# Cross-attention on one core: queries of two batches projected together with inner block products, context product plain, keys' affine folded into the queries'

## Chip, core and metric

The kernel runs on one NeuronCore of a Trainium2 chip. The metric is the device time in microseconds of one execution. Engines: TensorE (PE; its weight loads are shown apart as PEld), VectorE (DVE), ScalarE (ACT), GpSimd (POOL), and SyncE (SP), which issues nearly all DMA transfers. Each engine, SP's queue too, works through its instructions in the order in which the program lists them.

## The reference

64 batches of cross-attention, float32 throughout: x is (64, 256, 512), the context c is (64, 256, 384).

```python
text_p  = einsum('bld,dh->blh', x, W_text) + b_text        # queries, 512 -> 512
audio_p = einsum('bsd,dh->bsh', c, W_audio) + b_audio      # keys and values, 384 -> 512
Q = layer_norm(text_p, g1, beta1)
K = layer_norm(audio_p, g2, beta2)
V = audio_p
alpha = softmax(einsum('blh,bsh->bls', Q, K) / sqrt(512), axis=-1)
y = einsum('blh,hk->blk', einsum('bls,bsh->blh', alpha, V), W_out) + b_out
return layer_norm(y + x, g_out, beta_out)
```

## The kernel before

**Products.** A batch has five matrix products on TensorE. W_audio and W_out are folded once into `wao` (384 x 512), so the values are never formed: the context product takes the attention weights with the raw rows of c, and the output product takes that with `wao`.

- Keys (class `Thirds`): a scheme of 15 block products in place of 18 (weights 128x171), in methods `one` (2 products), `two` (2), `three` (1), `four` (5), `five` (5). They accumulate in PSUM areas M, L, T, U, N; between them VectorE and ScalarE move partial sums from area to area (`copy_n1`, `start_t`, `copy_t`, `start_l0`, `start_l1`, `take_m`, `start_u`). The sums of input blocks (`Sides`, tile csum) are made on GpSimd, one `cs[..].add(1)` each.
- Queries (class `Fork`): seven block products in place of eight (Strassen's idea in Winograd's form), each of two 128-row parts with 256 columns: methods `one` to `seven`. They share two PSUM banks (`fork`) with partial sums: `after_one`, `after_seven` and `seed` on ScalarE, `start_q3`, `step_r`, `after_five` on VectorE. `SumX` makes four sums of x blocks on GpSimd.
- Scores (class `Attention`): seven block products of 128 columns for eight (`score_part`), with sums of query and key blocks on GpSimd (`query_step`, `key_step`). Three batches at the start and two at the end use the plain product (`score`).
- Context: the first two of three 128-row groups of c by seven products of 128 columns (`z_part`, L1033) with sums `c_step` and `e_step` on GpSimd, copies `keep_z7`, `copy_z1`, `copy_top` on ScalarE, additions `add_u3`, `add_c22`, `add_c21` on VectorE; the third group plain (`context_two`, L1095).
- Output: the 15-product scheme again (object `y`), fed by `z_step` sums; its last sums (`plus_ends`, `plus_middle`, `plus_n0`, `last_..`) add x and give the row totals for the layer norm.

**Between products.** Queries and keys are normalised by rows on ScalarE (`square`, `scales_of`, `normalise`), stored to DRAM and fetched back as 32x32 squares (`store`, `fetch`: four transfers), so that VectorE's 32x32 transposes (`turn`) give their transposes; the attention weights go the same way (`store_e`, `fetch_e`, `turn_e`). x and c are fetched as squares as well (`turn_x`, `turn_c`). After the turn ScalarE applies gain and bias per column: four `affine_queries` and four `affine_keys` a batch (L527). The last layer norm is `totals`, `deviation`, `shift` (VectorE), `settle` (VectorE).

**Order.** The program is scheduled by hand: every method call is a line, and the lines of several batches are interleaved. The main loop runs over b = 3 to 60, one batch an iteration, and holds in one iteration the keys and queries of batch b+2, the scores of b, context and output of b-2, and the last layer norm of b-3. A long list of lines ahead of the loop and one after it treat the first and last batches. Score, context and third-group tiles share two PSUM banks in turn (`p_at`).

Of the kernel before, what the change touches and what calls it, by code (L numbers as in the profile page):

```python
# [22 lines left out]
def kernel(  # L23
# [34 lines left out]
    blk = ctx.enter_context(tc.tile_pool(name="blk", bufs=2))  # L58
    work = ctx.enter_context(tc.tile_pool(name="work", bufs=2))
# [26 lines left out]
    def load_x(b):  # L86
        xq = blk.tile([P, L // SQ, D // NQ], F32, tag="xq", name=f"xq_{b}")
        squares(xq, x[b])
        blocks[b].append(xq)
# [15 lines left out]
    make_identity(nc, ident)  # L105
    eps = const.tile([P, 1], F32, tag="eps", name="eps")
# [43 lines left out]
    blocks = {}  # L150
# [4 lines left out]
    columns = const.tile([P, 5, HC], F32, tag="columns", name="columns")  # L155

# [32 lines left out]
    class RowTurn:  # L189

        def __init__(self, rows_sb, chunks, name):
            self.rows, self.chunks = rows_sb, chunks
            tag = "yr" if chunks == DC else "kT"
            self.ar = work.tile([P, 2, chunks, P], F32, tag=tag, name=f"{name}r")
            self.T = work.tile([P, chunks, 2 * P], F32, tag=name, name=f"{name}_0")
# [8 lines left out]

    waT = []
# [75 lines left out]
    def weight_sums(w_sb, n, name):  # L281

        w = [[w_sb[:, j * n : (j + 1) * n, k * H2 : (k + 1) * H2] for k in (1, 0)] for j in (0, 1)]
        t = const.tile([P, 4, n, H2], F32, tag=name, name=name)
        add = nc.gpsimd.tensor_tensor
        add(t[:, 0], w[0][1], w[0][0], ALU.subtract)
        add(t[:, 1], w[1][1], t[:, 0], ALU.subtract)
        add(t[:, 2], w[1][1], w[0][1], ALU.subtract)
        add(t[:, 3], w[1][0], t[:, 1], ALU.subtract)
        ws = {1: w[0][0], 2: w[1][0], 3: w[1][1], 4: t[:, 3], 5: t[:, 0], 6: t[:, 1], 7: t[:, 2]}  # L290
        return {p: [ap[:, k, :] for k in range(n)] for p, ap in ws.items()}

    class SumX:

        def __init__(self, xT, engine=nc.gpsimd):
            n = DC // 2
            part = lambda i, j: xT[:, j * n : (j + 1) * n, bass.ts(i, P)]
            s = work.tile([P, 4, n, P], F32, tag="xsum", name="xsum")
            self.engine = engine
            self.steps = [  # L300
                (s[:, 2], part(0, 0), part(1, 0), ALU.subtract),
                (s[:, 0], part(1, 0), part(1, 1), ALU.add),
                (s[:, 1], s[:, 0], part(0, 0), ALU.subtract),
                (s[:, 3], part(0, 1), s[:, 1], ALU.subtract),
            ]
            ss = {
                1: part(0, 0), 2: part(0, 1), 4: part(1, 1),
                5: s[:, 0], 6: s[:, 1], 7: s[:, 2], 3: s[:, 3],
# [3 lines left out]
        def add(self, n=4):  # L312
# [114 lines left out]
    class Projection:  # L427
# [72 lines left out]
        def fetch(self):  # L500
            self.sq = blk.tile(
# [215 lines left out]
    class Fork(Projection):  # L717

        R, q1 = fork[0][:, :H2], fork[0][:, H2:]
        q2, q3 = fork[1][:, :H2], fork[1][:, H2:]  # L720
# [6 lines left out]
        @staticmethod  # L727
        def seed():
            nc.scalar.copy(Fork.R, bt_sb[:, H2:])

        def product(self, n, place):
            for c, (side, w) in enumerate(zip(self.sides[n], self.weights[n])):
# [4 lines left out]
                    start=(n == 7 and c == 0),  # L737
# [7 lines left out]
        def seven(self):  # L745
            self.product(7, self.q3)
# [4 lines left out]
        def after_seven(self):  # L751
            self.s7 = once.tile([P, H2], F32, tag="s7", name="s7")
            nc.scalar.copy(self.s7, self.q3)
# [4 lines left out]
        def start_q3(self):  # L758
            dve(self.q3, self.R, self.s7, ALU.add)

        def step_r(self):
            dve(self.R, self.R, bt_step, ALU.add)

        def after_six(self):
            self.start_q3()
            self.step_r()
# [4 lines left out]
        def after_five(self):  # L771
            dve(self.q2, self.R, self.s7, ALU.add)
# [7 lines left out]
        def four(self):  # L780
            self.product(4, self.q3)

        def rest(self):
            self.three()
            self.two()
            self.four()
# [18 lines left out]

    class Attention:
# [7 lines left out]
        def affine_queries(self, *chunks):  # L814
            self.q.affine(g1_sb, be1_sb, chunks or range(HC))

# [54 lines left out]
        def open_scores(self):  # L871

            self.sc = p_at.tile([P, LT, S], F32, tag="at", name="ps_sc")
            nc.vector.memset(self.sc[:, :, P:], 0.0)
# [91 lines left out]
        def fetch_e(self):  # L966
            self.sq = blk.tile([P, L // SQ, S // NQ], F32, tag="eq", name=f"eq_{self.b}")
# [18 lines left out]
        def context_sums(self):  # L986

            rows = c_rows[self.b]
            a = lambda j, s: rows[:, s, bass.ts(j, P)]
            t = once.tile([P, 3, P], F32, tag="asum", name="asum")  # L990
            self.csteps = [
                (t[:, 0], a(1, 0), a(1, 1), ALU.add),
                (t[:, 2], a(0, 0), a(1, 0), ALU.subtract),
                (t[:, 1], t[:, 0], a(0, 0), ALU.subtract),
                (a(1, 0), a(0, 1), t[:, 1], ALU.subtract),
            ]
            self.asides = {
                1: a(0, 0), 2: a(0, 1), 3: a(1, 0), 4: a(1, 1), 5: t[:, 0], 6: t[:, 1], 7: t[:, 2],
            }

        def weight_sums(self):

            t = once.tile([P, 4, P], F32, tag="esum", name="esum")
            b = lambda i, m: self.eT[:, i, bass.ts(m, P)]
            self.esteps = [
                (
                    t[:, 0:2],
                    self.eT[:, :, P:],
                    self.eT[:, 0].rearrange("p (m l) -> p m l", m=2),
                    ALU.subtract,  # L1010
                ),
                (t[:, 2], b(1, 1), t[:, 0], ALU.subtract),
                (t[:, 3], b(1, 0), t[:, 2], ALU.subtract),
            ]
            self.bsides = {
# [1460 lines left out]
```

## Time and profile before

| | |
|---|---|
| time, median of 3 runs | 1336.47 us (1336.44 to 1337.37) |
| span of the profiled execution, first to last instruction | 1333.9 us |
| what lies around the span, to the median of the runs | 2.6 us (the profiled execution's own time is not given beside its span) |
| PE busy | 1327.5 us, 8497 matmul records |
| PEld, DVE busy | 1246.6 us, 1257.0 us |
| ACT, POOL busy | 1174.8 us, 1172.8 us |
| granted TensorE clock | 1.000 |
| DMA | 322.23 MB, 242 GB/s |

The span is one execution. A float32 matmul appears as two records, as it passes through the array twice. In the groups of instructions a row gives line, engine, operation, output<-inputs, shapes, count, then busy time in us and the mean length of one in ns, then idle time ahead of it. The mean includes the part by which neighbours overlap, the busy time does not.

### The profile page before, as it was taken

The numbers are of one execution on the slowest core, as the hardware profiler recorded it, in microseconds if no ns is written. First come the engines' busy times: TensorE is split into PE (matmuls) and PEld (weight loads), VectorE is DVE, ScalarE is ACT, GpSimd is POOL, SyncE is SP. The second block draws the span as 40 slices with busy tenths as digits, with TensorE's granted clock in tenths as the row PEclk, the third lists the DMA queues.
The fourth block names the chain that finished last, engine by engine and source line by source line (L and its number), as shares of the span: only waits on it lengthen the run. The fifth ranks groups of instructions, "written<-read, shape, count | busy, mean of one in ns | idle before, by whom it ended". The sixth has DMA issues, their size and how long they took to land.

```text
span 1333.9 us, 29733 instructions
## 1 busy us (share of the span) xinstructions
PE 1327.5 (100%) x8497; PEld 1246.6 (93%) x8497; DVE 1257.0 (94%) x3314; ACT 1174.8 (88%) x3310; POOL 1172.8 (88%) x1854
## 2 busy tenths in 40 slices
PE   9999999999999999999999999999999999999998
PEld 5899999999999999999999999999999999999996
DVE  6769999999999999999999999999999999999977
ACT  4899898898898998998988988989988989889886
POOL 5789999999998998998999999989989989999964
PEclk9999999999999999999999999999999999999999
DMA  9988898898988988988888988988889888889783
GB/s 214 250 235 239 230 268 238 241 261 237 250 251 225 261 248 241 259 248 244 249 241 239 264 236 246 260 241 246 252 225 268 246 236 258 242 241 257 213 248 116
DMA packets 448970, 322.23 MB, mean 242 GB/s; under 512 B 153765, under 2 KB 381349, under 8 KB 448806
## 3 DMA queue, kind: packets, MB, share of 16 engines
q1 hardware_dynamic: 448710, 320.20, 85.7%
q8 instruction: 68, 1.11, 0.4%
q14 instruction: 96, 0.79, 0.2%
q10 hardware_dynamic: 96, 0.13, 0.0%
HBM read 203.57 MB, written 116.65 MB: 240 GB/s over the span
## 4 chain that ended last, share of the span: by engine, by line
PE 98%; DMA 1%; DVE 0%; SPq 0%; issue 0%; POOL 0%; ACT 0%; DVEq 0%
PE ps_f L733 29%; PE ps_m L557 16%; PE ps_sc L884 14%; PE ps_n L557 11%; PE ps_u L557 8%; PE ps_z L1033 7%; PE ps_l L557 5%; PE ps_z L1095 5%; PE ps_sc L823 1%; DMA ba<-in_L_xattn_b_audio_dram 0%; DMA c<-in_ctx_dram 0%; PE ps_l L244 0%; PE ps_f L440 0%; PE ps_fold L244 0%; PE ps_m L244 0%; PE ps_sc L900 0%
## 5 line engine op out<-in xcount | busy, mean ns | idle before, releaser
L352 POOL TENSOR_TENSOR csum<-csum,cT 128x256 f32<-128x256 f32 x310 | 202.0, 652 | 0.6
L733 PE MATMUL ps_f<-wtsum,xsum 128*128 128x256 f32 x756 | 194.0, 379 | 0.0
L527 ACT ACTIVATE qT<-qT,columns 128x256 f32<-128x256 f32 x256 | 152.9, 599 | 0.0
L733 PEld LDWEIGHTS ps_f<-wtsum,xsum 128*128 128x128 f32 x756 | 131.8, 191 | 11.4 <-issue 0.7
L869 POOL TENSOR_TENSOR qsum<-qT 128x256 f32<-128x256 f32 x118 | 86.4, 732 | 58.3 <-ACT qT L527 56.7
L1158 ACT ACTIVATE junk<-yr,nm 128x512 f32<-128x512 f32 x124 | 88.6, 715 | 55.0 <-POOL nm L1140 54.8
L527 ACT ACTIVATE kT<-kT,columns 128x256 f32<-128x256 f32 x256 | 133.7, 595 | 0.4 <-DVE kT L76 0.4
L884 PE MATMUL ps_sc<-kT,qT 128*128 128x128 f32 x928 | 131.8, 275 | 0.0
L733 PE MATMUL ps_f<-wt,xT 128*128 128x256 f32 x504 | 129.5, 379 | 0.0
L1357 DVE SCALAR_TENSOR_TENSOR yr<-yr,rstd,beo 128x512 f32<-128x512 f32 x120 | 123.0, 1025 | 0.1
L884 PEld LDWEIGHTS ps_sc<-kT,qT 128*128 128x128 f32 x928 | 121.3, 192 | 0.0
L1348 DVE SCALAR_TENSOR_TENSOR yr<-yr,nm,go 128x512 f32<-128x512 f32 x124 | 109.7, 885 | 0.0
L794 ACT ACTIVATE junk<-ps_f 128x512 f32<-128x512 f32 x126 | 75.2, 597 | 35.7 <-PE ps_f L733 32.2
L884 PEld LDWEIGHTS ps_sc<-ksum,qsum 128*128 128x128 f32 x696 | 100.6, 191 | 6.0
L884 PE MATMUL ps_sc<-ksum,qsum 128*128 128x128 f32 x696 | 105.8, 275 | 0.0
L733 PEld LDWEIGHTS ps_f<-wt,xT 128*128 128x128 f32 x504 | 88.4, 190 | 6.7
L314 POOL TENSOR_TENSOR xsum<-xT 128x256 f32<-128x256 f32 x124 | 91.0, 735 | 1.9 <-DVE xT L76 1.9
L541 DVE TENSOR_TENSOR ps_l<-ps_m,t 128x171 f32<-128x171 f32 x248 | 82.8, 334 | 8.7 <-ACT t L605 3.0
L520 DVE STREAM_TRANSPOSE kT<-kq 128x512 f32<-128x512 f32 x122 | 85.4, 702 | 2.0 <-DMA kq<-kd 2.0
L488 ACT ACTIVATE kr<-kr,rstd 128x512 f32<-128x512 f32 x126 | 84.7, 727 | 0.0
L460 ACT ACTIVATE junk<-kr 128x512 f32<-128x512 f32 x126 | 80.9, 642 | 0.3
L804 ACT ACTIVATE qr<-ps_f,rstd 128x512 f32<-128x512 f32 x126 | 80.2, 690 | 0.2
(302 smaller groups left out, 4670.1 us busy)
## 6 DMA issues: line engine op xcount, KB each, us to landing
kd<-kr SPq DMA_DIRECT2D x64, 512.0 KB, 3.4
kq<-kd SPq DMA_DIRECT2D x256, 128.0 KB, 3.8
qd<-qr SPq DMA_DIRECT2D x64, 512.0 KB, 3.2
qq<-qd SPq DMA_DIRECT2D x256, 128.0 KB, 4.3
xq<-in_x_dram SPq DMA_DIRECT2D x252, 128.0 KB, 2.8
x<-in_x_dram SPq DMA_DIRECT2D x63, 512.0 KB, 5.0
out_dram<-yr SPq DMA_DIRECT2D x62, 512.0 KB, 3.8
cq<-in_ctx_dram SPq DMA_DIRECT2D x252, 96.0 KB, 2.4
```

What stands on the lines that cost most here:

```text
L314: self.engine.tensor_tensor(*step)
L352: nc.gpsimd.tensor_tensor(*step)
L520: nc.vector.transpose(self.T.rearrange("p k (q t j) -> p t q k j", t=self.nt, j=SQ)[:, t], self.sq[:, t * NQ : (t + 1) * NQ].rearrange("p ...
L527: nc.scalar.activation(self.T[:, k, :], self.T[:, k, :], AF.Identity, bias=bet[:, k : k + 1], scale=gam[:, k : k + 1],)
L557: nc.tensor.matmul(place, lhsT=self.sides.of[n], rhs=self.weights[n], start=(n == 14), stop=True, skip_group_check=True,)
L733: nc.tensor.matmul(place, lhsT=side, rhs=w, start=(n == 7 and c == 0), stop=True, skip_group_check=True,)
L869: nc.gpsimd.tensor_tensor(*self.steps[n])
L884: nc.tensor.matmul(self.place(t, m), lhsT=self.qsides[n][:, c], rhs=self.ksides[n][:, c], start=False, stop=True, skip_group_check=True,)
L1033: nc.tensor.matmul(self.zp[{1: 0, 2: 0, 4: 2}.get(n, 1)], lhsT=self.asides[n], rhs=self.bsides[n], start=(n == 7), stop=True, skip_group_c ...
L1158: nc.scalar.activation(junk, self.y[:, t, :], AF.Square, bias=self.nm[:, t : t + 1], accum_out=self.ssq[:, t : t + 1],)
L1348: nc.vector.scalar_tensor_tensor(row, row, self.nm[:, t : t + 1], go_sb, ALU.add, ALU.mult)
L1357: nc.vector.scalar_tensor_tensor(self.y[:, t, :], self.y[:, t, :], self.r[t], beo_sb, ALU.mult, ALU.add)
```

## The change

- Batches 6 to 63 are projected in pairs (class `Pair`); batches 1 to 5 keep `Fork`, which now uses another form of the same scheme. Of the seven products of a pair three (2, 3, 4) are `whole`: two batches, two parts, 256 columns. The other four (1, 5, 6, 7) are done by seven inner products each, 128 columns wide (`multiply(m, n)`), with sums of sides on GpSimd (`sum`, `side`), inner sums of weights made once (`inner_weights`), and, for each of the four, a `seed`, a `spread` and a `keep` on ScalarE and two `plus` on VectorE. Between the products lie `keep_v`, `keep_s7` and three `leave` (ScalarE), `raise_v`, two `plus_v` and `leave_11` (VectorE). The rows of the queries go to SBUF before `square` and `normalise`.
- The context product is plain for all batches (`context_part`, `copy_one`): no `z_part`, `c_step`, `e_step`, and none of the copies and additions with them.
- From batch 3 on the keys get no affine, up to the last two batches: the queries' gain and bias are multiplied by the keys' gain (`both`, `affine_both`). What the keys' bias would add is the same for all keys of a query and drops out of the softmax.
- The main loop runs over b = 4, 6, .. 58, two batches an iteration. In it one of the two `settle` of a batch becomes `scale_row` (ScalarE) and `lift_rows` (GpSimd), and `open_scores` clears with ScalarE in place of a memset on VectorE.
- The landing rooms of fetched queries, keys and attention weights (tags qq, kq, eq) have one buffer in place of two; the transposed x lies in one fixed room for two batches (`X`), and the sums of both in `xsums`.
- The lists of lines ahead of, in and after the loop are in a new order.

```diff
-            self.sq = blk.tile(
+            self.sq = sq1.tile(
...
+    class Pair:
+
+        A, B = [f.rearrange("p (i h) -> p i h", i=2) for f in fork]
+        room = xsums.rearrange("p i n c l -> p (i n c l)")
+        T = room[:, : 3 * H].rearrange("p (n i c l) -> p n i c l", n=3, i=2, c=2)
+        I = room[:, 3 * H : 3 * H + 3 * P].rearrange("p (n l) -> p n l", n=3)
+        x00, x01 = X[:, :, 0:2, :P], X[:, :, 2:4, :P]
+        x10, x11 = X[:, :, 0:2, P:], X[:, :, 2:4, P:]
+        bank = {1: A, 7: A, 6: B, 5: B}
+        sides = {1: x00, 5: T[:, 0], 6: T[:, 1], 7: T[:, 2], 2: x01, 3: x11, 4: x10}
...
+        def sum(self, n):
+            o, i0, i1 = {
+                1: (self.T[:, 0], self.x10, self.x00),
+                3: (self.T[:, 2], self.x11, self.x10),
+                2: (self.T[:, 1], self.x11, self.T[:, 0]),
+                4: (self.x10, self.x01, self.T[:, 1]),
+            }[n]
+            nc.gpsimd.tensor_tensor(o, i0, i1, ALU.subtract)
+
+        def side(self, m, k):
+            y = self.sides[m]
+            o, i0, i1 = [
+                (self.I[:, 0:2], y[:, 1], y[:, :, 0]),
+                (self.I[:, 2], y[:, 1, 1], self.I[:, 0]),
+                (y[:, 1, 0], y[:, 0, 1], self.I[:, 2]),
+            ][k]
+            nc.gpsimd.tensor_tensor(o, i0, i1, ALU.subtract)
...
+        def multiply(self, m, n):
...
+            i, j = {7: (1, 1), 2: (0, 0), 4: (0, 1)}.get(n, (1, 0))
+            nc.tensor.matmul(
+                self.place(m, i, j), lhsT=side, rhs=wt_parts[m][n], start=False, stop=True, skip_group_check=True
+            )
+
+        def spread(self, m):
+            nc.scalar.copy(self.place(m, 0, 0), self.place(m, 1, 0))
...
+        def plus(self, m, i):
+            dve(self.place(m, i, 1), self.place(m, 1, 0), self.i7, ALU.add)
+
+        def whole(self, m, i):
+            bank = self.B if m == 3 else self.A
+            for c in range(2):
+                nc.tensor.matmul(
+                    bank[:, i],
+                    lhsT=self.sides[m][:, i, c],
+                    rhs=wt_pairs[m][c],
...
+        def leave(self, i, j):
+            nc.scalar.copy(self.rows[:, :, i, j * H2 : (j + 1) * H2], self.B if i else self.A)
+
+        def raise_v(self):
+            dve(self.v, self.B, self.v, ALU.add)
+
+        def plus_v(self, bank):
+            dve(bank, bank, self.v, ALU.add)
...
+        def affine_both(self, *chunks):
+            self.q.affine(both[:, 0], both[:, 1], chunks or range(HC))
...
-            nc.vector.memset(self.sc[:, :, P:], 0.0)
+            nc.scalar.mul(self.sc[:, :, P:], bt_sb[:, :H2].rearrange("p (t m) -> p t m", t=LT), 0.0)
...
-    for b in range(3, B - 3):
+    for b in range(4, B - 4, 2):
...
+        f.multiply(5, 5)
+        k2.start_l1()
+        old.z_step(2)
+        cs[b + 3].add(1)
+        k2.four()
+        old.z_step(7)
+        f.leave(0, 1)
+        settled.shift(1)
+        f.plus(5, 1)
+        f.multiply(5, 2)
+        k2.take_m()
+        settled.shift(0)
...
+        f.multiply(5, 3)
+        at1.affine_both(1)
+        at.open_scores()
+        k2.start_u()
+        f.plus_v(f.B)
+        at1.affine_both(2)
+        k2.five()
...
+        at.store_e()
+        at1.score_part(1, 7)
...
+        q[b + 2].fetch()
+        k[b + 2].turn([1])
+        settled.store()
+        s.whole(2, 0)
...
+        y1.three()
+        s.keep(7)
+        s.spread(7)
+        att[b + 2].q.turn()
...
+        q[b + 3].fetch()
```

More of the change, by code (lines that the diff above doesn't have):

```diff
@@ L1971 @@
[L1971 to L1988 removed]
+        f.keep(5)
@@ L2335 @@
+    at.multiply(0, bank[5])
+    end.affine_keys(0)
     old.o.last_00()
[L2336 to L2353 removed]
+    end.score(0, 1)
+    end.start_output('kq')
```

2265 lines of the change are left out of this document (1388 added, 877 removed).

## The prediction

> **What bounds the kernel now.** I read the page first (busy shares, the chain that ended last), then busy time by stretch, then the chain in order of time inside one steady stretch, then the groups of instructions by shape, and last the order of time on VectorE and TensorE around one wait.
>
> ```profile
> span 1333.9 us, 29733 instructions
> PE 98%; DMA 1%; DVE 0%; SPq 0%; issue 0%; POOL 0%; ACT 0%; DVEq 0%
> ...
> core 0: us, PE busy (x) PEld busy (x) DVE busy (x) ACT busy (x) POOL busy (x), PEclk, DMA share, GB/s
> 0.00:50.00 50.00, 48.38 (x178) 30.49 (x179) 35.85 (x69) 27.57 (x67) 33.01 (x58) 1.00 0.96 231
> 600.00:800.00 200.00, 200.00 (x1321) 191.19 (x1320) 195.30 (x526) 179.88 (x513) 181.73 (x287) 1.00 0.87 245
> 1300.00:1334.00 34.00, 29.09 (x139) 23.05 (x137) 26.05 (x67) 20.25 (x52) 16.30 (x23) 0.98 0.35 120
> ```
>
> TensorE carries 98% of the chain and has no idle time in the steady stretch, at full granted clock. The other engines are near it: 97.6% VectorE, 90% ScalarE, 91% GpSimd. A busy PE can hide a slow one, so I need the spacing of matmuls, which the chain gives (each piece starts where the one before it ends):
>
> ```profile
> 600.09 0.86 PE ps_f L733 x4
> 605.60 0.29 PE ps_u L557 x2
> 605.88 0.89 PE ps_sc L884 x8
> ```
>
> A product of two 128-row blocks is two records (float32 goes through twice). A record 256 columns wide is spaced 0.86/4 = 0.216 us, one of 128 columns 0.89/8 = 0.111, one of 171 columns 0.145. Cost follows columns: 0.84 to 0.87 ns per column and record at every width. One batch before has 32 records of 256 (28 query, 4 context), 42 of 128 (28 score, 14 context) and 60 of 171 (keys and output): 6.91 + 4.66 + 8.70 = 20.27 us. The real period:
>
> ```profile
> L874 DVE MEMSET ps_sc<- x58: 272/272/272, 97.6 to 1254.9; 128x256 f32 x58
> ```
>
> (1254.9 - 97.6)/57 = 20.30 us. So in the loop the time is the matmuls' spacing and nothing else, and a change moves the time by the columns it removes, as long as TensorE is still fed.
>
> **The change on TensorE.** How many records there are of each kind now:
>
> ```profile
> L733 PE MATMUL ps_f<-wtsum,xsum 128*128 128x256 f32 x756 | 194.0, 379 | 0.0
> L733 PE MATMUL ps_f<-wt,xT 128*128 128x256 f32 x504 | 129.5, 379 | 0.0
> ...
> L1033 PE MATMUL ps_z<-eT,c 128*128 128x128 f32 x354 | 68.3, 275 | 0.0
> L1033 PE MATMUL ps_z<-esum,asum 128*128 128x128 f32 x354 | 68.0, 274 | 0.0
> L733 PE MATMUL ps_f<-wt,xsum 128*128 128x256 f32 x252 | 64.7, 379 | 0.0
> L733 PE MATMUL ps_f<-wtsum,xT 128*128 128x256 f32 x252 | 64.7, 379 | 0.0
> ...
> L1033 PE MATMUL ps_z<-esum,c 128*128 128x128 f32 x118 | 22.8, 275 | 0.0
> ```
>
> Queries: 756 + 504 + 252 + 252 = 1764 records, 28 for each of 63 batches. After, batches 6 to 63 go as 29 pairs. A pair has three whole products (2, 3, 4) of 8 records of 256, and four (1, 5, 6, 7) of seven inner products, 2 records of 128 each: 24 x 0.216 + 56 x 0.111 = 5.18 + 6.22 = 11.40 us, where two batches now take 56 x 0.216 = 12.10. Saved 0.70 us a pair, 29 times: -20.2 us.
>
> Context: 354 + 354 + 118 = 826 records, 14 for each of 59 batches. The plain product puts 8 records of 256 in their place: 8 x 0.216 - 14 x 0.111 = 1.73 - 1.55 = +0.17 us, 59 times: +10.3 us. Keys, output and scores keep their products, so TensorE's work falls by 9.9 us, 0.35 us for an iteration of two batches (40.6 to 40.25). Against the profiled execution's own span that is 1333.9 - 9.9 = 1324.0; the median of the runs (1336.47) lies 2.6 above the span, so the floor as timed is 1326.6.
>
> **The change on the other engines**, per iteration of two batches. Prices are busy time divided by count (or the mean where neighbours don't overlap):
>
> ```profile
> L527 ACT ACTIVATE kT<-kT,columns 128x256 f32<-128x256 f32 x256 | 133.7, 595 | 0.4 <-DVE kT L76 0.4
> L729 ACT COPY ps_f<-bt 128x256 f32<-128x256 f32 x63 | 24.1, 383 | 2.8 <-DVE kr L449 2.8
> L927 ACT COPY ps_sc<-ps_sc 128x128 f32<-128x128 f32 x58 | 15.8, 272 | 0.0
> L1111 ACT COPY zT<-ps_z 128x512 f32<-128x512 f32 x5 | 2.9, 587 | 1.2 <-PE ps_z L1095 1.0
> L1362 ACT ACTIVATE yr<-yr,rstd 128x512 f32<-128x512 f32 x4 | 2.7, 716 | 0.1
> ...
> L1357 DVE SCALAR_TENSOR_TENSOR yr<-yr,rstd,beo 128x512 f32<-128x512 f32 x120 | 123.0, 1025 | 0.1
> L541 DVE TENSOR_TENSOR ps_f<-ps_f,s 128x256 f32<-128x256 f32 x126 | 49.0, 389 | 3.1 <-PE ps_f L733 2.8 <-ACT s L753 0.3
> L541 DVE TENSOR_TENSOR ps_sc<-ps_sc,sc 128x128 f32<-128x128 f32 x117 | 34.2, 293 | 9.5 <-PE ps_sc L884 8.5 <-PE ps_sc L900 1.0
> L449 DVE TENSOR_TENSOR kr<-ps_f,ba 128x512 f32<-128x512 f32 x2 | 1.3, 676 | 0.0
> ...
> L314 POOL TENSOR_TENSOR xsum<-xT 128x256 f32<-128x256 f32 x124 | 91.0, 735 | 1.9 <-DVE xT L76 1.9
> L1020 POOL TENSOR_TENSOR asum<-c 128x128 f32<-128x128 f32 x118 | 53.9, 457 | 0.0
> L866 POOL TENSOR_TENSOR ksum<-kT 128x512 f32<-128x512 f32 x59 | 75.4, 1278 | 1.5 <-ACT kT L527 1.4
> L1366 POOL TENSOR_TENSOR yr<-yr,beo 128x512 f32<-128x512 f32 x4 | 5.1, 1275 | 4.2 <-ACT yr L1362 4.2
> ```
>
> ScalarE loses 8 scalings of the keys (8 x 0.522), 8 copies of 256 (three of each Fork, and the top of the context; 0.383) and 4 of 128 (0.272): -8.3 us. It gains 6 fills of 256 (four seeds, two openings of the scores), 8 copies of 128 (spread, keep), 7 of 512 (keep_v, keep_s7, three leave, two copy_one; 0.58) and 2 scale_row (0.675): +9.9. Net +1.6, from 0.90 x 40.6 = 36.5 to 38.1 us of 40.25. The fills become multiplications from SBUF, which no row shows writing PSUM; at the 256-wide key scaling's full 0.595 they add 1.3 more (39.4), at a copy's price nothing. I take the copy's price, the same shape and target.
>
> VectorE loses 6 additions of 256 (start_q3, step_r, after_five; 0.389), 6 of 128 (add_c21, add_c22, add_u3; 0.293), 2 memsets (0.272) and 2 settle (1.025): -6.7. It gains 8 `plus` of 128 and 4 additions of 512 (raise_v, two plus_v, leave_11; 0.676): +5.0. Net -1.6, from 39.6 to 38.0.
>
> GpSimd loses 8 sums of 256 for x, and the context's 12 of 128 and 2 of 256: 7.4 + 5.5 = 12.8 at those rows, more where a sum waits for the one before it. It gains 4 sums of 512, 4 sides of 256 and 8 of 128, 2 lift_rows: 5.1 + 2.9 + 3.7 + 2.5 = 14.2. At most +1.4, from 36.9 to 38.3.
>
> So each engine still has less work than TensorE's 40.25. DMA moves the same bytes in the same number of transfers; only the landing rooms of queries, keys and exponentials go from two to one, which is the third rival. The removed key scaling hides nothing and hurts nothing by itself: ScalarE's time is off the chain (0%). GpSimd's 16 inner sums of the weights (16 x 0.457 = 7.3 us) come once, in the first 100 us, spread between other sums; TensorE idled only 1.6 us in the first 50 and 4.9 in the last 34. Both ends are reordered; I bound what that does at 4 us either way, most of the idle time that is there to win, and take 0.
>
> **Feeding TensorE.** What can't be summed is whether the orders fit. The tightest place that I find by hand in the loop is k2.four, k2.five of the first half. Before, as it runs:
>
> ```profile
> 608.55 0.34 DVE L541 TENSOR_TENSOR m<-ps_m,ba_delta 128x171 f32<-128x171 f32 x1
> 608.92 0.34 DVE L541 TENSOR_TENSOR ps_u<-ps_m,m 128x171 f32<-128x171 f32 x1
> 609.17 0.74 DVE L1348 SCALAR_TENSOR_TENSOR yr<-yr,nm,go 128x512 f32<-128x512 f32 x1
> 616.68 1.04 DVE L1348 SCALAR_TENSOR_TENSOR yr<-yr,nm,go 128x512 f32<-128x512 f32 x1
> ...
> 608.35 0.74 PE L557 MATMUL ps_l<-wa_thirds,cT 128*128 128x171 f32 x4
> 608.93 0.74 PE L557 MATMUL ps_n<-wa_thirds,csum 128*128 128x171 f32 x4
> 609.51 0.74 PE L557 MATMUL ps_m<-wa_thirds,cT 128*128 128x171 f32 x4
> ```
>
> Products into M end at 608.35 (where those into L begin); take_m starts 0.20 later, start_u ends at 609.26, and the next product into M, which must wait for it, goes at 609.51: 0.25 us to spare. After, TensorE has two inner products more in between (+0.44), so the room is 1.16 + 0.44 = 1.60 us; VectorE has settled.shift(0) between take_m and start_u, 0.74 to 1.04 us by the two rows. Its chain grows from 609.26 - 608.35 = 0.91 to about 0.91 + 0.66 (0.74 less the 0.08 by which neighbours overlap) = 1.57, or to 1.87. That is between 0.03 to spare and 0.27 us of stall an iteration. I take 0.07 (nearer the lower end, since VectorE has 1.6 us less to do and can come early): 28 x 0.07 = 2 us. Forecast 1326.6 + 2 = 1328.6.
>
> **The rivals.**
> First, the other side: that VectorE queue decides. If shift(0) and the work queued in front of it bring start_u late by one long shift (1.04) in each iteration, products into M wait, all of TensorE behind them too, and the time is 1326.6 + 28 x 1.04 = 1355.7, slower than before. It turns from gain to loss where the wait passes 0.35 us an iteration. For it: the 0.03 us of room above; VectorE's share stays at 38.0/40.25 = 94%. Against it: before, at 97.6%, the same place runs with 0.25 us to spare. The Trainium skill (GPSIMD Engine Reference, Specifications) says that GpSimd shares its SBUF interface with VectorE instructions that read two SBUF tensors. The spread from 0.74 to 1.04 fits that, and the lift_rows that the change adds would then push toward the long end. Chance 0.15.
>
> Second, half of that: the stalls add up to about the saving and nothing measurable is left, 28 x 0.35 us, 1336.4. Chance 0.12.
>
> Third, a transfer that is no longer hidden. With one room, the even batch's queries can be fetched only after the odd one's were turned, and they are turned soon after:
>
> ```profile
> qq<-qd SPq DMA_DIRECT2D x256, 128.0 KB, 4.3
> ```
>
> Between that fetch and its turn TensorE has whole(2,0), three score parts, two inner products, y1.one, two, three: 0.86 + 1.33 + 0.44 + 1.45 = 4.1 us, against 4.3 to land, though SP may issue it some 2 us earlier, as soon as the store of the exponentials is out. If it lands 1 us late and VectorE passes all of that on, 28 us: 1354.6. It is not hidden only if SP comes late too. Chance 0.04.
>
> Fourth, narrow products that don't halve, so that the inner scheme does not do what it says:
>
> ```profile
> L884 PEld LDWEIGHTS ps_sc<-kT,qT 128*128 128x128 f32 x928 | 121.3, 192 | 0.0
> ```
>
> A weight load lasts 0.192 us, longer than the 0.111 spacing. Were the inner products spaced by it, 29 x 56 x (0.192 - 0.111) = +131 us, 1458. The score row above speaks against it: 8 records of that width, each with its own load, in 0.89 us. The Trainium skill (TensorE: Matmul & The Clock Gate, Back-to-back issue gap) has loads and matmuls together set the spacing, 81 ns at 128 columns and 131 at 512; an estimate on a line between these puts 128 columns at 0.83 of 256, and the pair at 15.2 us instead of 11.4, a loss of 90 us. This trace disagrees: 0.51. Chance 0.01.
>
> **How the numbers follow.** A measurement of this kernel can tell about 0.2%, 2.7 us, from no change. TensorE fed but for small waits, and so faster, has 0.68; its own range is 1323 (floor less most of the ends' 4 us) to 1333. The second rival, same, 0.12; the first, third and fourth, slower, 0.15 + 0.04 + 0.01 = 0.20. The range must reach into the slower cases until 0.1 is left above: half of the first rival's stall, 28 x 0.65 = 18 us over the floor, 1345.
>
> **What would show it.** Right: loop period 40.3 us for two batches, records of the inner products spaced 0.11, 0.86 us for four of the whole ones, TensorE idle nowhere in the loop, ScalarE near 95% and VectorE near 94% of it. Wrong: gaps in front of the products into M or in front of k2.three (VectorE reaches start_t last there, after y1's last sums, plus_v and turn_c), VectorE waiting for qq, or ends longer than now by several us.

## The result and the profile after

The changed kernel is slower: 1369.39 us median (1368.19 to 1370.41) against 1336.45 (1336.12 to 1337.37), ratio 1.0246 [1.0231, 1.0260]. The forecast was 1328.6 us, faster.

The page after: its head, the engines' busy times, and the shares of the chain that ended last.

```profile
span 1367.8 us, 30175 instructions
...
PE 1341.2 (98%) x8839; PEld 1249.3 (91%) x8839; DVE 1236.8 (90%) x3191; ACT 1209.4 (88%) x3391; POOL 1192.1 (87%) x1745
...
PE 73%; ACT 19%; issue 2%; DVE 2%; DMA 2%; POOL 1%; SPq 0%; DVEq 0%; ACTq 0%; POOLq 0%
```

The chain now runs through ScalarE for 19% of the span; before it did so for 0%. That share misleads, as the timeline below shows. The view by stretches of time has, in each row, the stretch, its length, and the busy time of TensorE, its weight loads, VectorE, ScalarE and GpSimd, then the granted clock:

```profile
100.00:200.00 100.00, 97.75 (x655) 91.22 (x654) 88.28 (x229) 85.73 (x243) 88.97 (x129) 1.00 0.82 224
600.00:800.00 200.00, 196.88 (x1346) 186.84 (x1345) 187.30 (x496) 181.38 (x514) 179.27 (x261) 1.00 0.88 244
1200.00:1300.00 100.00, 98.77 (x672) 93.85 (x671) 94.03 (x249) 91.50 (x256) 88.97 (x131) 1.00 0.87 242
```

TensorE stands still in every stretch of the loop, at full clock. No other engine is full either: between 600 and 800 us VectorE has 94%, ScalarE 91%, GpSimd 90%.

To size the stops better than the busy time does (a record's modelled end covers part of a stop), take the start of each matmul record less the start of the one ahead of it, and take off the spacing of that width as it runs undisturbed: 0.111 us for 128 columns, 0.145 for 171, 0.216 for 256, 0.429 for 512. What is left is a gap. Every gap given below is such a difference, a mean over some 25 iterations of the loop. The spacings alone come to 1322.5 us before and 1312.6 after; that is 9.9 less, as forecast. The rest of the span is 11.4 us before and 55.2 after: 43.8 more, and 43.8 - 9.9 is the 33.9 by which the span grew. Between 200 and 1200 us the gaps are 32.0 us (before: 1.3), between 100 and 200 they are 5.9 (0.2), in the first 50 us 5.5 (3.4), behind 1200 us 4.9 (0.2). The loop's period is 41.53 us for two batches; its floor is 40.25. So 1.28 us is lost in each of 28 iterations on average, some 36 us.

Two thirds of it lies in one place, at the head of the second half. The view of waits gives engine and line, what it waited for, the total in us, how often, and the longest:

```profile
PEld ps_u L573 <- DVE ps_u L557: 21.9, 27, 0.8
...
PEld ps_n L573 <- DVE yr L723: 8.0, 28, 0.3
```

The product into ps_u is k21.three, 0.75 us late on average and 0.10 more between its two records; what it waits for is VectorE's start_t. The second row is k21.one behind the last sums of the batch before (0.15 in all). Smaller gaps stand ahead of s.multiply(1, 5) (0.10) and k2.one (0.07). The timeline there has the start, the duration, and in brackets the idle time and what ended it:

```profile
228.43 0.50 DVE L723 SCALAR_TENSOR_TENSOR yr<-ps_l,x 128x342 f32<-128x342 f32 x1
228.85 1.86 DVE L1440 SCALAR_TENSOR_TENSOR yr<-yr,rstd,beo 128x512 f32<-128x512 f32 x1
230.64 0.32 DVE L723 SCALAR_TENSOR_TENSOR yr<-ps_u,u 128x170 f32<-128x170 f32 x1
...
230.89 0.08 DVE L723 DVE_READ_ACCUMULATOR yr<-ps_u,u 128x1 f32 x1
231.07 0.34 DVE L557 TENSOR_TENSOR ps_u<-ps_n,n 128x171 f32<-128x171 f32 x1
...
229.35 0.29 ACT L610 COPY n<-ps_n 128x171 f32<-128x171 f32 x1
...
228.89 1.28 POOL L864 TENSOR_TENSOR X<-X,xsums 128x512 f32<-128x512 f32 x1
230.12 1.72 POOL L1017 TENSOR_TENSOR ksum<-kT 128x512 f32<-128x512 f32 x1
...
230.46 0.39 PE L889 MATMUL ps_f<-wt_inner,xsums 128*128 128x128 f32 x2
231.47 0.56 PE L573 MATMUL ps_u<-wa_thirds,csum 128*128 128x171 f32 x2 [0.62 <-DVE ps_u L557]
```

L1440 is settled.settle(0). It takes 1.86 us here, beside GpSimd's new sum of 512 columns, s.sum(4), and key_step(0), which itself takes 1.72 where 1.28 is its usual time. Behind the settling wait last_00 and start_t, and behind start_t the products. ScalarE is not what start_t waits for: the copy that it reads, n, is done at 229.64, and start_t begins 0.10 us behind the accumulator read of last_00. In most iterations the view of the chain names ScalarE's copy into zT there, since that copy ends just then; but copy_one, which makes it, stands behind start_t in the program, so start_t can't be waiting for it.

Over the whole run the instruction took, shortest, median and longest in ns:

```profile
L1440 DVE SCALAR_TENSOR_TENSOR yr<-yr,rstd,beo x62: 720/968/1879, 125.0 to 1344.9; 128x512 f32<-128x512 f32 x62
```

In the loop it has two prices: 1.85 to 1.88 us at this place, 0.95 to 0.97 at the odd batch's settling. One iteration is an exception, and it tests the reading without any edit. There GpSimd's s.sum(4) is the one that is stretched:

```profile
395.35 0.75 DVE L1440 SCALAR_TENSOR_TENSOR yr<-yr,rstd,beo 128x512 f32<-128x512 f32 x1
395.41 1.83 POOL L864 TENSOR_TENSOR X<-X,xsums 128x512 f32<-128x512 f32 x1
```

The gap ahead of k21.three is missing there, and from this settling to the next one it is 40.56 us, where it is 41.54 just ahead.

The place that the prediction held for the tightest, k2.four to k2.five of the first half, runs as hoped:

```profile
215.02 0.34 DVE L557 TENSOR_TENSOR m<-ps_m,ba_delta 128x171 f32<-128x171 f32 x1
215.27 0.74 DVE L1431 SCALAR_TENSOR_TENSOR yr<-yr,nm,go 128x512 f32<-128x512 f32 x1
215.93 0.34 DVE L557 TENSOR_TENSOR ps_u<-ps_m,m 128x171 f32<-128x171 f32 x1
...
213.50 0.38 PE L889 MATMUL ps_f<-wtsum,xsums 128*128 128x128 f32 x2
213.72 0.39 PE L889 MATMUL ps_f<-wt_inner,xsums 128*128 128x128 f32 x2
213.94 0.46 PE L573 MATMUL ps_u<-wa_thirds,csum 128*128 128x171 f32 x2
...
215.84 0.74 PE L573 MATMUL ps_n<-wa_thirds,csum 128*128 128x171 f32 x4
216.42 0.74 PE L573 MATMUL ps_m<-wa_thirds,cT 128*128 128x171 f32 x4
```

The shift takes 0.74, start_u ends at 216.27, and the product into M goes at 216.42, right behind the four records ahead of it (215.84 + 4 x 0.145). The same rows show the inner products two records in 0.22 us, as priced.

### The profile page after: what moved, and what is told of

The parts are those of the page before. It is cut to its first block, busy times and chain, and to the rows that moved or that the text cites. A ratio compares the mean times of both kernels' runs of the same rounds, so it can differ in the third digit from the quotient of the medians.

```text
span 1367.8 us, 30175 instructions
## 1 busy us (share of the span) xinstructions
PE 1341.2 (98%) x8839; PEld 1249.3 (91%) x8839; DVE 1236.8 (90%) x3191; ACT 1209.4 (88%) x3391; POOL 1192.1 (87%) x1745
## 4 chain that ended last, share of the span: by engine, by line
PE 73%; ACT 19%; issue 2%; DVE 2%; DMA 2%; POOL 1%; SPq 0%; DVEq 0%; ACTq 0%; POOLq 0%
PE ps_f L889 12%; PE ps_m L573 11%; PE ps_f L906 11%; PE ps_sc L1035 9%; PE ps_z L1175 8%; PE ps_n L573 7%; PE ps_u L573 7%; PE ps_l L573 4%; ACT junk L938 4%; ACT kr L504 3%; ACT qr L944 2%; ACT junk L476 2%; PE ps_f L749 2%; ACT e L1097 2%; PE ps_sc L974 1%
## 5 line engine op out<-in xcount | busy, mean ns | idle before, releaser
L368 POOL TENSOR_TENSOR csum<-csum,cT 128x256 f32<-128x256 f32 (+1 forms) x310 | 213.2, 696 | 7.4
L1175 PE MATMUL ps_z<-eT,c 128*128 128x256 f32 x768 | 196.8, 379 | 0.0
L873 POOL TENSOR_TENSOR xsums<-xsums 128x128 f32<-128x128 f32 (+1 forms) x261 | 143.6, 550 | 51.1 <-PE ps_f L889 48.5
L1175 PEld LDWEIGHTS ps_z<-eT,c 128*128 128x128 f32 x768 | 135.6, 190 | 10.3
L889 PE MATMUL ps_f<-wt_inner,xsums 128*128 128x128 f32 x696 | 137.2, 279 | 0.9 <-DVE ps_f L557 0.5
L543 ACT ACTIVATE qT<-qT,both 128x256 f32<-128x256 f32 x236 | 134.3, 593 | 0.0
L889 PE MATMUL ps_f<-wtsum,xsums 128*128 128x128 f32 x696 | 120.3, 275 | 0.0
L889 PEld LDWEIGHTS ps_f<-wt_inner,xsums 128*128 128x128 f32 x696 | 111.9, 190 | 8.6 <-DVE ps_f L557 1.1
L906 PE MATMUL ps_f<-wt,X 128*128 128x256 f32 x464 | 114.6, 380 | 0.0
L889 PEld LDWEIGHTS ps_f<-wtsum,xsums 128*128 128x128 f32 x696 | 106.3, 191 | 6.0 <-DVE ps_f L557 0.7
```

What stands on the lines that cost most here:

```text
L368: nc.gpsimd.tensor_tensor(*step)
L543: nc.scalar.activation(self.T[:, k, :], self.T[:, k, :], AF.Identity, bias=bet[:, k : k + 1], scale=gam[:, k : k + 1],)
L873: nc.gpsimd.tensor_tensor(o, i0, i1, ALU.subtract)
L889: nc.tensor.matmul(self.place(m, i, j), lhsT=side, rhs=wt_parts[m][n], start=False, stop=True, skip_group_check=True)
L906: nc.tensor.matmul(bank[:, i], lhsT=self.sides[m][:, i, c], rhs=wt_pairs[m][c], start=False, stop=True, skip_group_check=True,)
L1175: nc.tensor.matmul(ps, lhsT=c_rows[self.b][:, s, bass.ts(j, P)], rhs=self.eT[:, s, :], start=start, stop=(s == ST - 1), skip_group_check=True,
```

## The experiments

The theory: the columns are saved as worked out, and VectorE's order at the head of k21 gives back more than that, because a settling stands ahead of start_t and GpSimd's sums stretch it. Rivals: the plain context product or the folded affine costs time; VectorE's load as such is too high; the ends of the program lose the time.

**One part alone: the plain context in the kernel before.** `z_part` and its sums leave, `context_part` comes at the places of the products.

> The kernel before with one part of the change alone: the context product plain (four records pairs of 256 columns where seven of 128 were), without the sums, copies and additions that went with it. If time follows the columns of TensorE: 59 x 0.174 us = +10.3 us, 1346.7. If the engines freed by it had held something up, less; if the plain product waits for its operands in that order, more.

Measured 1347.19 us (1346.43 to 1347.52) against 1336.74, ratio 1.0076 [1.0061, 1.0092]: 10.5 us, by 10.3 of the sum. TensorE has no gap in it:

```profile
600.00:800.00 200.00, 200.00 (x1253) 189.83 (x1252) 186.83 (x490) 178.68 (x487) 138.27 (x215) 1.00 0.86 247
```

GpSimd, the last of the busy times, has 138 us of 200 to do, some 43 less than before, and nothing comes of it: columns alone set the time here.

**One part alone: the keys' affine folded into the queries'.** `affine_keys` goes, `affine_queries` becomes `affine_both`, in the kernel before.

> The kernel before with another part alone: the keys' gain and bias folded into the queries' affine from batch 3 to 61, so that ScalarE has four scalings of 0.52 us less per batch. TensorE has the same work, ScalarE's time was off the chain: no change, 1336.5 within 1 us. If ScalarE's load had any part in the time, up to 2 us x 58 less.

Measured 1337.16 us (1335.77 to 1337.76), ratio 1.0001 [0.9991, 1.0010]. No effect clear of the noise, so these two parts, each taken alone, account for none of the loss beyond the columns.

**The settling behind start_l0.**

```diff
         y.last_01(x_old)
-        settled.settle(0)
...
         k21.start_l0()
+        settled.settle(0)
```

> The changed kernel with one line of the loop moved: settled.settle(0) goes from in front of y.last_00 to behind k21.start_l0. Theory (VectorE queue at the start of the second half): settle(0) takes 1.86 us there while GpSimd sums 512 columns, start_t behind it comes 0.75 us late, and TensorE stands still in front of k21.three in each of 28 iterations. Then that gap goes, and most of the 1.28 us of stall in an iteration of 41.53: 0.8 to 1.1 us x 28 = 22 to 31 us, a time of 1338 to 1347. Rival (the loads of ScalarE, VectorE and GpSimd together are too much, and the wait only moves): within 5 us of 1369.

Measured 1356.91 us (1356.35 to 1357.60), ratio 1.0150 [1.0135, 1.0165]; 12.5 us of the loss are gone, about half of what was expected and more than the rival allows. The gap ahead of k21.three is gone, and a smaller one stands ahead of k21.four's product into M (0.48 + 0.10):

```profile
229.27 0.34 DVE L557 TENSOR_TENSOR ps_l<-ps_m,t 128x171 f32<-128x171 f32 x1 [0.33 <-ACT t L621]
229.52 0.74 DVE L1440 SCALAR_TENSOR_TENSOR yr<-yr,rstd,beo 128x512 f32<-128x512 f32 x1
...
230.45 0.33 DVE L557 TENSOR_TENSOR ps_l<-ps_m,t 128x171 f32<-128x171 f32 x1
...
231.72 0.34 DVE L557 TENSOR_TENSOR m<-ps_m,ba_delta 128x171 f32<-128x171 f32 x1 [0.62 <-PE ps_m L573]
...
230.06 0.46 PE L573 MATMUL ps_u<-wa_thirds,csum 128*128 128x171 f32 x2
230.83 0.85 PE L573 MATMUL ps_m<-wa_thirds,csum 128*128 128x171 f32 x4 [0.32 <-DVE ps_l L557]
```

The settling takes 0.74 here, where GpSimd stands idle for nearly half of it, and now start_l1 comes late by that much. Behind it VectorE waits 0.62 us for the late product into ps_m, at take_m.

**GpSimd's sums later, VectorE's order left alone.** `key_step(0)` goes behind `s.side(6, 0)`, `s.sum(4)` behind `at1.query_step(2)`.

> The changed kernel with VectorE's order untouched and two GpSimd lines of the loop moved later: key_step(0) behind side(6,0), s.sum(4) behind at1.query_step(2), so that GpSimd does nothing while settle(0) runs. If the two engines block each other, settle(0) falls from 1.86 us to about 0.75 at its old place, the gap in front of k21.three goes, and the time falls by 20 us or more, less what GpSimd's later sums cost at the end of the half (up to 0.5 us x 28 = 14). If settle(0) is long for another reason, or its length does not matter, it stays at 1.8 us or the time stays within 5 us of 1369.

Measured 1385.82 us (1385.69 to 1386.29), ratio 1.0367 [1.0351, 1.0382]. The price of the settling falls to 0.83 us at most, as expected, and the gap ahead of k21.three is gone:

```profile
L1440 DVE SCALAR_TENSOR_TENSOR yr<-yr,rstd,beo x62: 722/749/830, 124.5 to 1361.0; 128x512 f32<-128x512 f32 x62
```

With the same order on VectorE, the stretching is thus GpSimd's doing. The time, expected to fall, rises by 16.4 us, since what GpSimd does later is missed: the scores wait 0.46 + 0.10, y1.one 0.42 + 0.10, and two other products 0.29 and 0.25:

```profile
236.78 0.71 PE L1035 MATMUL ps_sc<-kT,qT 128*128 128x128 f32 x4 [0.30 <-ACT ps_sc L1025]
...
241.63 0.56 PE L573 MATMUL ps_n<-wao,zsum 128*128 128x171 f32 x2 [0.26 <-POOL zsum L1164]
```

**The settling ahead of k21.take_m,** in that wait of 0.62 us.

```diff
         at1.query_step(1)
+        settled.settle(0)
         k21.take_m()
```

> The changed kernel, with VectorE's settled.settle(0) of the loop moved ahead of k21.take_m, to where VectorE stands idle for 0.50 to 0.62 us for the product into ps_m. Theory (the lost time is the queue of VectorE at the start of the second half: a settling that GpSimd's sums stretch, ahead of the work that the products of k21 wait for): both the gap ahead of k21.three (0.75 us plus 0.10) and the one ahead of k21.four's product into M (0.48 plus 0.10, with the settling behind start_l0) go; 28 iterations by 0.58 us less than the 1356.9 us of the run with the settling behind start_l0: some 1340 to 1342 us, the loop's period 40.5 to 40.7 us. Rival (VectorE's load as such is too much, and any place for the settling only moves the gap): the products wait elsewhere for about as long, 1355 to 1360 us.

**And two stages begun later,** in the same place.

```diff
+        f.multiply(5, 1)
         k2.one()
...
+        s.multiply(1, 7)
+        s.multiply(1, 1)
         k21.one()
```

> As the run with the settling ahead of k21.take_m, and in TensorE's order f.multiply(5, 1) moved ahead of k2.one, and s.multiply(1, 7) and s.multiply(1, 1) ahead of k21.one, which gives VectorE's last sums about 0.22 and 0.44 us more before the products that wait for them (0.104 plus 0.046 us ahead of k21.one's second product, 0.068 ahead of k2.one). Theory (the slack between VectorE's last sums and the products of the next stage is what is short): these stalls go too, 28 by 0.2 us less than its neighbour, a period of 40.3 to 40.4 us and some 1333 to 1336 us, which is at or just under the kernel before. Rival (VectorE is so far behind that later products wait instead): no less than its neighbour's time, 1340 us or more.

Measured 1362.06 us (1360.84 to 1362.51), ratio 1.0190 [1.0176, 1.0204], and 1362.60 (1362.38 to 1362.86), 1.0195 [1.0181, 1.0209]. Both expectations missed; the times lie near the rivals' figures. In the first the gap stands ahead of k21.five's product into M (0.66 + 0.10):

```profile
231.39 1.32 DVE L1440 SCALAR_TENSOR_TENSOR yr<-yr,rstd,beo 128x512 f32<-128x512 f32 x1
232.63 0.32 DVE L557 TENSOR_TENSOR m<-ps_m,ba_delta 128x171 f32<-128x171 f32 x1
232.99 0.34 DVE L557 TENSOR_TENSOR ps_u<-ps_m,m 128x171 f32<-128x171 f32 x1
...
231.43 0.73 POOL L1020 TENSOR_TENSOR qsum<-qT 128x256 f32<-128x256 f32 x1
232.11 1.18 POOL L1017 TENSOR_TENSOR ksum<-kT,ksum 128x256 f32<-128x256 f32 x1
...
233.39 0.85 PE L573 MATMUL ps_m<-wa_thirds,cT 128*128 128x171 f32 x4 [0.50 <-DVE ps_u L557]
```

VectorE's wait of 0.62 us for ps_m belongs to the run with the settling behind start_l0, and that run's gap made it: in the changed kernel itself VectorE mostly waits 0.2 us there, and 0.1 with the settling left out (below). With the gap gone TensorE comes sooner and there is nothing to fill; the settling lies beside key_step and takes 1.32. In the second kernel the gaps of k21.one and k2.one are gone, but the products behind begin 0.14 us behind ScalarE's seed and keep, and no sooner: as much is lost in new gaps (0.25) as was won.

**The settling behind all of k21; the settling left out; the settling on the two other engines.**

```diff
         k[b + 2].turn([1])
+        settled.settle(0)
         settled.store()
```

> The changed kernel, with the loop's first settled.settle(0) moved far back, to just ahead of settled.store(), behind the whole of k21, where VectorE stands idle for 0.38 us and GpSimd for 0.71 us. Theory (it is the place that costs: between k21.one and k21.five VectorE's queue has no room for a settling of 0.72 to 1.86 us, and behind k21 it has some): both gaps, ahead of k21.three and ahead of k21's products into M, go; what VectorE does next, the adding of the scores and y1's first terms, comes 0.35 us late at most; the period is 40.5 to 40.9 us and the time 1338 to 1350 us. Rival (VectorE's load as such, 94% of the loop, is too much and the products wait wherever the settling stands): 1355 to 1362 us, as at the two other places.

> The changed kernel without the loop's first settled.settle(0): row tile 0 of the even batches is stored without its last scaling and bias, and VectorE has one instruction of 0.72 to 1.86 us less in an iteration. It shows the most that any place for this instruction can bring. Theory (this one instruction is the cause of the gap ahead of k21.three and of its followers): the period is 40.45 us, the floor of 40.25 and the 0.15 to 0.22 us ahead of k21.one and k2.one, and the time 1334 to 1338 us, where the kernel before stands. Rival (the whole order is too tight on VectorE, and something else is late next): 1345 us or more.

> The changed kernel, with the loop's first settled.settle(0) done by the two other engines, as its row tile 1 is: scale_row(0) on ScalarE behind at.divide_e([0]), where ScalarE stands idle 0.60 us, and lift_rows(0, 1) on GpSimd where that stands idle 0.71 us, ahead of s.side(7, 0), with the store behind it. Theory (VectorE's queue is what is short; the two others have room): the gaps ahead of k21's products go; side(7, 0) comes 0.57 us late, which its products may or may not notice: a period of 40.4 to 40.9 us, 1335 to 1350 us. Rival (GpSimd, with 1.28 us more, is late next or stretches VectorE's other instructions): a new gap ahead of s.multiply(7, 7) or ahead of y1's products, 1350 us or more.

Measured 1346.61 us (1345.41 to 1348.20), 1.0073 [1.0060, 1.0087]; left out 1340.69 (1340.52 to 1341.06), 1.0031 [1.0020, 1.0043]; on the other engines 1354.95 (1354.75 to 1355.57), 1.0137 [1.0123, 1.0151]. So one instruction of VectorE in an iteration is worth 1369.4 - 1340.7 = 28.7 us, and its place alone 22.8. The load as such is not the main cause: behind k21 the same instruction costs 5.9 us, 0.21 an iteration, where the scores wait for add_p7(0):

```profile
236.59 0.78 DVE L1440 SCALAR_TENSOR_TENSOR yr<-yr,rstd,beo 128x512 f32<-128x512 f32 x1
237.30 0.29 DVE L557 TENSOR_TENSOR ps_sc<-ps_sc,sc 128x128 f32<-128x128 f32 x1
...
236.96 0.75 PE L573 MATMUL ps_n<-wao,zsum 128*128 128x171 f32 x4
237.64 0.71 PE L1035 MATMUL ps_sc<-kT,qT 128*128 128x128 f32 x4
```

Without the settling the chain that ended last is TensorE's for 96% and ScalarE's for 0%, and the time is 3 us above what was expected; gaps of 0.15 ahead of k21.one and 0.06 ahead of k2.one, and the ends, are left. On the other engines the time is one that the rival allows, but neither theory nor rival names the gap that came: it stands ahead of at1.score_part(1, 7) (0.26 + 0.10), behind scale_row(0) on ScalarE, which holds up open_scores; a smaller one stands ahead of a later score part (0.07 + 0.10). ScalarE's idle 0.60 us, which scale_row was to fill, is found in the two runs with the settling ahead of take_m, next to their gap; in the changed kernel, and with the settling left out, ScalarE has none there.

**Three handovers eased, and ScalarE's order with them.**

```diff
+        f.multiply(5, 1)
         k2.one()
...
+        s.multiply(1, 1)
         k21.one()
...
         at1.add_p7(0)
+        settled.settle(0)
+        settled.store()
```

> As the run with the settling ahead of settled.store(), and three steps for the gaps that are left in it: the settling and the store stand behind at1.add_p7(0), which the scores wait for (0.21 us an iteration); s.multiply(1, 1) stands ahead of k21.one, which waits 0.15 us for VectorE's last sums of the batch before, and f.multiply(5, 1) ahead of k2.one, which waits 0.06 us. Theory (after the settling's place, these handovers between VectorE's last sums and the next stage are what is left): 29 by 0.35 to 0.42 us less than 1346.6, some 1334 to 1338 us, period 40.3 to 40.4 us. Rival (TensorE is let go too early and then waits for ScalarE, whose order has seed, spread and keep behind exponentials; this happened with both first products moved): 1340 us or more.

> As its neighbour, with ScalarE's order in front of k21 eased as well: s.seed(1) ahead of k2.normalise, f.normalise(0, 1) and the queries' store behind k21's first copies, and s.multiply(1, 7) too ahead of k21.one. Theory (ScalarE's queue is full from k2's squares to old1.product_sums, and seed, copy_n1, spread and keep come late in it): copies come 0.3 to 0.7 us sooner, no gap is left at k21.one or behind it, period 40.25 to 40.35, 1331 to 1336 us, at or under the kernel before. Rival (the queries come back later by the move and VectorE waits for them at their turn, or ScalarE is late behind k21): 1340 us or more, with a gap in front of y1 or of the scores.

Measured 1364.37 us (1363.00 to 1366.74), 1.0211 [1.0197, 1.0225], and 1379.01 (1377.85 to 1380.08), 1.0318 [1.0304, 1.0332]. Each is slower than the kernel that it starts from, and the first shows its rival's time but not its rival's mechanism. The gaps ahead of k21.one, k2.one and the scores are gone in the first, and one of 0.86 + 0.10 stands ahead of y1.three instead:

```profile
238.96 1.27 DVE L1440 SCALAR_TENSOR_TENSOR yr<-yr,rstd,beo 128x512 f32<-128x512 f32 x1
240.15 1.21 DVE L1431 SCALAR_TENSOR_TENSOR yr<-yr,nm,go 128x512 f32<-128x512 f32 x1
...
241.68 0.33 DVE L557 TENSOR_TENSOR ps_u<-ps_n,n 128x171 f32<-128x171 f32 x1
...
242.06 0.56 PE L573 MATMUL ps_u<-wao_thirds,zsum 128*128 128x171 f32 x2 [0.70 <-DVE ps_u L557]
```

Two instructions that GpSimd can stretch stand behind each other, and y1's start_t behind both. That is 18 us more than with the settling ahead of settled.store(). The second kernel has that gap too (0.83 + 0.10) and others of some 0.5 us together at scores and k21's products; its moves, taken together, cost 14.6 us more.

**The settling ahead of k21.middle_v,** with the two products moved as above.

```diff
+        settled.settle(0)
         k21.middle_v()
```

> The changed kernel with s.multiply(1, 1) ahead of k21.one and f.multiply(5, 1) ahead of k2.one, which did away with those two gaps (0.15 and 0.06 us an iteration) in the run with the settling behind at1.add_p7(0), and with settled.settle(0) ahead of k21.middle_v, where VectorE stands idle 0.49 us for ScalarE's copy u, and where no shift stands next to it. Theory (an instruction that GpSimd can stretch costs nothing where VectorE waits anyway and the products behind have 0.5 us to spare): no gap over 0.1 us in the loop, period 40.3 to 40.4 us, some 1333 to 1337 us, at the kernel before or just under it. Rival (GpSimd's key_step and side stretch the settling past 1.2 us there, k21's last rows and its keys' turn come late, and y1.one or the scores wait): 1342 to 1355 us.

Measured 1340.44 us (1339.15 to 1341.23), 1.0030 [1.0019, 1.0040]: 29 us of the 33 are back, 3 us short of what was expected. VectorE's idle time of 0.49 us at this place stands in the changed kernel and also with the settling left out, so no gap of k21 made it. The one larger gap that is left, 0.20, comes from a sum of GpSimd that the settling stretches in its turn, side(6, 1), 0.90 us instead of 0.46; s.multiply(6, 6) waits for it:

```profile
232.08 1.02 DVE L1440 SCALAR_TENSOR_TENSOR yr<-yr,rstd,beo 128x512 f32<-128x512 f32 x1
...
232.51 0.90 POOL L873 TENSOR_TENSOR xsums<-xsums 128x128 f32<-128x128 f32 x1
...
233.15 0.39 PE L889 MATMUL ps_f<-wtsum,xsums 128*128 128x128 f32 x2
233.47 0.49 PE L889 MATMUL ps_f<-wt_inner,xsums 128*128 128x128 f32 x2
```

**That gap, by TensorE's order and by GpSimd's.** In the first kernel `s.multiply(6, 6)` goes behind `s.whole(2, 1)`, past `s.plus(6, 0)`, so that this sum lacks the product. In the second `s.side(6, 1)` goes ahead of `key_step(2)`.

> As the run with the settling ahead of k21.middle_v, and s.multiply(6, 6), which waits 0.20 us there for GpSimd's side(6, 1), behind s.whole(2, 1). Theory (that wait is the last of the loop's gaps, and the work behind it has room): 28 by 0.2 us less than 1340.4, some 1334.8 us, period 40.3 us. Rival (whole(2, 1) then waits for ScalarE's keep_v, or keep(6) and plus(6, 0) come late, and the ends hold the rest): 1338 us or more.

> As the same run, with GpSimd's s.side(6, 1) ahead of key_step(2) instead of behind it, so that it lies ahead of the settling that stretches it (0.90 us there, 0.46 elsewhere). Theory (the gap is GpSimd's sum, late by its place in the queue): the same gain, some 1335 us. Rival (key_step(2), 0.5 to 0.9 us later, makes the scores of k21's neighbour wait instead): 1338 to 1350 us, with a gap ahead of score_part(1, 7).

Measured 1363.53 us (1362.63 to 1363.89), 1.0202 [1.0188, 1.0216], and 1338.45 (1337.56 to 1339.68), 1.0016 [1.0008, 1.0025]. In the first the product waits 0.90 us at its new place, for VectorE's plus(6, 0): a miss. The second closes the gap, but half of it goes to the scores (0.12), and the time is at the lower end of the rival's range, 3 us above what was expected:

```profile
600.00:800.00 200.00, 200.00 (x1387) 192.01 (x1386) 188.76 (x504) 185.91 (x528) 185.07 (x267) 1.00 0.89 247
```

Four lines moved in the loop bring the changed kernel from 1369.4 to 1338.5 us, still 2 us over the kernel before; no version beat it. What is left is 6.5 us of gaps between 200 and 1200 us, 2.7 between 100 and 150, 1.8 between 1250 and 1300 and 1.2 more than before in the first 50 us. That the change would win without these follows from the sum alone; it was not run.

## Why the prediction was wrong

Right, by its own steps. The columns: 9.9 us less, to the tenth. The context's share: 10.3 forecast, 10.5 measured alone. The folded affine: nothing, as said. The other engines' loads, below TensorE's: in the last kernel, whose period is 40.46 us, VectorE has 38.2 us of work an iteration, ScalarE 37.6 and GpSimd 37.4, by its row above, where 38.0, 38.1 and at most 38.3 were forecast. The fourth rival is out, since the inner products run at 0.11 us a record, and so is the third: no wait of VectorE for the queries' transfer is among the gaps. (Its sum counts two inner products between fetch and turn where the loop has three, so 4.3 us and not 4.1; nothing follows from it.) The second rival is out by size: the stops come to four times the saving.

Wrong: the term for feeding TensorE, put at 0.07 us an iteration. It was 1.28. That step failed in two ways.

First, one place was examined, and the whole term read from it. That place has no gap. The text itself named k2.three, "after y1's last sums, plus_v and turn_c", as what would show it wrong; the gap stood at its twin in the second half, k21.three, with the settling among those last sums. That place was never priced.

Second, the settling was priced at its mean of 1.025 us and as load, not as something that stands in a queue with a product behind it. The kernel before already shows that this mean mixes different prices:

```profile
L1357 DVE SCALAR_TENSOR_TENSOR yr<-yr,rstd,beo x120: 709/877/1217, 106.5 to 1309.8; 128x512 f32<-128x512 f32 x120
```

Its price was no property of the instruction: 0.72 to 1.88 in the changed kernel, by what GpSimd does beside it. The change puts four sums of 512 columns an iteration on GpSimd, and the last of them, with key_step behind it, falls on the settling.

The first rival had the mechanism: VectorE's queue decides, and a gain turns into a loss from 0.35 us of stop an iteration on. It had the wrong instruction (the shift), the wrong half, and 1.04 us for 1.28. It was given 0.15 because the kernel before had 0.25 us to spare at the place that was looked at. The rule cited there (the Trainium skill, GPSIMD Engine Reference, Specifications: the SBUF interface is shared, with contention for VectorE instructions with two SBUF inputs) agrees with these runs: the settling takes 1.86 us beside s.sum(4), 0.74 where GpSimd is idle for nearly half of it, and never over 0.83 once GpSimd's sums are moved. The page gives no size. The prediction used the rule for the shift alone, where it cost nothing.

The ends were taken as 0 within 4 us. They cost some 6, and why is not shown: in the last kernel, with the loop's gaps mostly closed, 10.0 us of gaps lie outside 200 to 1200 us, before 3.8.

The upper end of the range was called half of the first rival's stall, but its 0.65 us is not half of 1.04; with 0.52 it would be 1341. The measured time lies above either.

The chance of 0.68 rested on loads: each engine had less to do than TensorE. All of that held, and TensorE still stood still, because an order written by hand has to fit at every handover.

## What to carry to other kernels

When a change keeps an engine below its load and reorders its queue, list each handover to the bound engine, and for each write down what stands ahead of it in the queue, at its longest price and not at its mean. An idle time next to a gap may be made by the gap, and then it goes when the gap goes (twice here); see first whether it is still there in a run without the gap, as the 0.49 us ahead of middle_v was. An instruction that another engine can stretch belongs where the products behind it have slack, and not next to a second one of its kind.

## What the runs showed of the hardware that was not expected

The size of the contention, and that it goes both ways. A VectorE scalar_tensor_tensor of 128x512 fp32 with two SBUF inputs takes 0.75 us where GpSimd works beside it for a tenth of the time (the run with GpSimd's sums later) and up to 1.88 beside GpSimd tensor_tensors. GpSimd's own take longer too: 1.72 for 1.28 at 512 columns, 1.18 for 0.73 at 256, 0.90 for 0.46 at 128, each about 0.45 us more, and 1.83 for 1.28 in the one iteration in which the settling was short. Why GpSimd gave way that once is not shown: the settling starts 0.03 to 0.06 us ahead of the sum there as elsewhere. So a settling can hold up a product through GpSimd as well as through VectorE.
